# Building one quad's left factors later, reordering the last quad, and moving the weight sums in a two-layer graph kernel

## The chip, the cores and the metric

The kernel runs on one core of one Trainium2 chip. The metric is the device time of one execution in microseconds (us). Three runs of the kernel before took 2237.49, 2238.95 and 2239.25 us; their median, 2238.95, is the number against which the changed kernel stands. A further execution was taken by the hardware profiler; all lines of the trace come from it.

Five engines work side by side, each through its own list of instructions in order: TensorE (PE in the profile; PEld is its loading of stationary operands), VectorE (DVE), ScalarE (ACT), GpSimd (POOL) and SyncE (SP), which here only issues DMA transfers. POOL and ACT issue some transfers too.

## The reference

128 graphs, each with 128 nodes of 512 features, go through two layers. Everything is float32. Cut to what matters:

```python
# layer 0
h  = relu(layernorm(x))
Xw = h @ Wv + bv
e  = leaky_relu(sj[:, None, :] + si[:, :, None] + ab)      # sj, si = Xw @ the halves of aw
transition = adj * exp(e), each row divided by its sum
H = 0; Xk = h
for k in range(3):
    H  = H + Xk @ Wk[k] + bk[k]
    Xk = transition @ Xk
x = x + relu(H)
# layer 1
h    = relu(layernorm(x))
q, k = split(h @ Wqk);  v = h @ Wv
agg  = adj @ (k * mask)
w    = mask * sum(q * agg, axis=-1) / sqrt(512)            # one score per node
x    = x + softmax(w, over the nodes)[:, :, None] * v
```

The graphs don't touch each other. In layer 1 the scores of a graph need the product with the query and key weights, and the scaled values need the scores of the whole graph.

## The kernel before, in words

**Tiling.** Layer 0 goes over the graphs in 64 pairs (p = 0 to 63, some 21.6 us each), layer 1 in 32 quads (q = 0 to 31, two pairs each, some 24.5 us). A layer's large products are done by Strassen's scheme: a 2x2 block product with 7 block products instead of 8, from sums of blocks of the left operand and sums of blocks of the right one. Layer 1 uses the scheme twice, one inside the other: seven *outer* factors, numbered 1 to 7, each itself a product of seven *inner* ones. The outer factor's left operand is a sum of blocks of the normalised, transposed rows; the weight's sum is its right operand. PE's banks are eight tiles in PSUM, a1, b1, c1, e1 (set 1) and a2, b2, c2, e2 (set 2).

**Three kinds of preparation in layer 0.**

*Weight sums.* Layer 1's right operands are made once. In pairs 5 to 8, one VectorE step of 128x1024 each makes the outer sums (`combine_steps(*OUTER)`, tile `tl`). In pairs 9 to 15, one outer factor per pair, four steps of 128x256 (`prepare`, `combine_steps`, line 191, tile `stage`) make its four inner sums; `store_all` then puts them into DRAM (`rwd`) by four transfers on SP. From pair 16 on they are loaded back (`rw`). Where steps stand in VectorE's order is set by the main loop: with four steps, the first two stand in the `middle` of `statistics` of pair p+3 (behind its aggregate, ahead of the rest of its short arithmetic), the last two behind `for_layer1`, right ahead of the combination `x` (line 629) that ends the pair. A single step, in pairs 5 to 8, stands in that last place as well.

*Normalised rows for layer 1.* At the end of a pair `norm2` normalises the pair's result on ACT, stores it in DRAM (`h2d`) and has it loaded back in blocks of 32 rows (`by_blocks`: four loads of 128 KB on SP, tile `hv`). The blocks are there for a transposition: VectorE transposes 32x32 blocks, so that rows loaded in block order come out as a transposed tile.

*Left factors.* One pair later `for_layer1` transposes the blocks of that pair into `fw` (line 429, four transposes of 128x256). When both pairs of a quad are there, it makes the outer left factors: two sums, a store of the first half of the eight slots to DRAM (`fd`); then, in `upper`, two more sums and a store of the second half. The upper sums are made at the next quad's first pair. The stores are issued by POOL, except the second half of quad 30 and both halves of quad 31, which SP issues; quad 30's second half is slipped between the store of pair 63's rows and their load as blocks (`LAST`). In layer 1 `load_left` loads these factors back, 2 MB a quad, one quad ahead.

**What sets the order.** In layer 0 the kernel gives edges: `behind(what, op)` puts an operation behind the last one of that name (`tc.issue_after(done[what])`); all else follows the program's order and the data. In layer 1 each engine's list is the recorded order of calls: `put` chains every operation to the one before it on its engine (`dve`, `act`, `pool`, `sync`, `swdge`). PE's order is fixed by `ordered` in both layers.

**A quad of layer 1.** Two `one_round`s run side by side, one per bank set: in the first half of the quad the outer factors (1, 5) and (2, 6), in the second half (3, 7) and (4). A round has seven steps (products 1, 5, 6, 2, 7, 3, 4 with their copies and adds), and `together` runs the pair of rounds step by step; after step i it runs the work hooked to i. Into these hooks go the inner left sums of this quad (LATE) and the next one (EARLY), the loads of the next quad's rows and adjacency (`load_rest`), the softmax of the quad before (`peaks`, `exp_own`, `exp`, `factors`), the scaling of values by the softmax (`scale`, ACT), the addition of the residual (`add_x1`, a DMA that adds, issued by POOL) and the stores. `catch_up` opens a quad with the scores of the quad before and the loads of the next left factors. SBUF space comes from four pools `back[0]` to `back[3]`.

**The last quad** has an order of its own, written out by hand from line 1125 on: two rounds with two factors, (1, 6) and (2, 7), then the single factors 4, 5 and 3, with work of quads 29 and 30 in between. There its own scores, softmax and stores must follow quickly, for nothing else is left to cover them. The operations `u2`, `on_p5` and `from_u2` put part of the adding of factors onto POOL.

Of the kernel before, what the change touches and what calls it, by code (L numbers as in the profile page):

```python
# [16 lines left out]
def kernel(  # L17
# [28 lines left out]
    P = 128  # L46
# [287 lines left out]
    def by_blocks(h, hd=None, between=None):  # L334

        hd = dram.tile([G, P, D], FP, name="hd") if hd is None else hd
        nc.sync.dma_start(hd.rearrange("g n d -> n g d"), h)
        if between:
            between()
        hv = front.tile([P, G, Q, P], FP, name="hv")  # L340
        v = hd.rearrange("g (q b) (c i) -> c b (g q) i", b=S32, i=P)
        for c in range(DC):
            at = hv[c * S32:(c + 1) * S32].rearrange("p g q i -> p (g q) i")
            done["hv"] = nc.sync.dma_start(at, v[c]).ins  # L344
        return hv
# [69 lines left out]
    SUMS, LAST = {}, []  # L415

    def for_layer1(p):
# [13 lines left out]
        if second:  # L431
# [3 lines left out]
            def store_half(i):  # L435
                queue = nc.gpsimd if q + 1 + i < NQ else nc.sync
                half = slice(4 * i, 4 * i + 4)
                queue.dma_start(fd[:, half].rearrange("p o n -> p (o n)"), fv[:, half].rearrange("p o n -> p (o n)"))  # L438

            def upper():  # L440
                behind("c12", nc.vector.tensor_sub, at[7], at[1], fv[:, L21])
                done["c12"] = nc.vector.tensor_sub(at[3], at[2], at[6]).ins
                if q == NQ - 2:
                    LAST.append(partial(store_half, 1))
                else:
                    store_half(1)
# [5 lines left out]
            if q + 1 == NQ:  # L452
                SUMS.pop(q)()
# [179 lines left out]
    def norm2(p):  # L633

        if p not in RS2:
            norm2_statistics(p, "s7")
        rs = RS2.pop(p)
        h = behind("s7", norm_relu, X1[p], rs=rs)
        done["h2"] = done["h"]
        HV2[p] = by_blocks(h, H2D[p], LAST.pop() if p == NP - 1 else None)  # L640
# [60 lines left out]
    def inner_sums(q, factors, space=None):  # L701
# [3 lines left out]
        s = (space or early).tile([P, 4, n, N], FP, name=f"in{first}")  # L705
# [43 lines left out]
    for p in range(NP):  # L749
# [7 lines left out]
        def between():  # L757
            if p == 0:
                behind("t", norm0, 2)
                behind("rs", begin, 1)  # L760
                return
            if p + 2 < NP:
                behind("t", begin, p + 2)
            if p + 3 < NP:
                two = weights[:2] if len(weights) > 2 else []
# [15 lines left out]
        if p > 0:  # L781
            behind("c12", for_layer1, p - 1)
        for step in weights[-2:]:
            behind("c12", step)
            done["c12"] = done["right"]
# [51 lines left out]
    for_layer1(NP - 1)  # L837


# [31 lines left out]
    load_left(1, swdge)  # L871

# [163 lines left out]
    def catch_up(q, spread=True):  # L1036

        if q + 1 < NQ:
            load_left(q + 1, sync, (0,))
        scores(q - 1, 1, C[q - 1][:, 2])  # L1040
        if spread:
            PW[q - 1] = spread_scores(W[q - 1])
        if q + 1 < NQ:
# [23 lines left out]
    for q in range(NQ - 1):  # L1067
        if q:
# [5 lines left out]

        together(one_round(q, set1, (1, 5), s1, plain_ends(lambda i, j: c[:, 0:2, i, j])),
# [4 lines left out]
                  2: lambda: load_rest(q + 1, sync),  # L1080
                  3: work(*([lambda: scale(late, 1, 0)] if q > 1 else []),
# [14 lines left out]
        hooks = {3: sums[:2], 4: sums[2:]}  # L1096
# [16 lines left out]
        if q == NQ - 2:  # L1113
            sums = inner_sums(NQ - 1, LATE, back[3])
# [6 lines left out]
        if q > 1:  # L1121
            store(late, 1)
            C.pop(late)

# [7 lines left out]
    catch_up(q, False)  # L1132
# [9 lines left out]
    def u2(i, j):  # L1142
        pool(nc.gpsimd.tensor_add, c_(1, i, j), c_(0, i, j), c_(1, i, j))

    def on_p5(i):
        pool(nc.gpsimd.tensor_add, c[:, 2:4, i, 1], c[:, 0:2, i, 1], s2[:, 0].rearrange("p (k d) -> p k d", k=2))

    def from_u2(i, j):
        return lambda bank: dve(nc.vector.tensor_add, c[:, 2:4, i, j], bank, c[:, 0:2, i, j])

    def on_top(i, j):
        return lambda bank, t: in_place(c[:, 2:4, i, j])(bank)

    ra = one_round(q, set1, (1, 6), s1, plain_ends(lambda i, j: c[:, 0:2, i, j]), direct=True)
    rb = one_round(q, set2, (2, 7), s2, {(0, 0): from_u2(0, 0), (1, 1): on_top(1, 1), (0, 1): on_top(0, 1),
                                         (1, 0): from_u2(1, 0)}, direct=True)

    def a_h2(g):

        pair, j = divmod(g, 2)  # L1160
        bank = (a1, b1, c1, e1)[g]
# [14 lines left out]
    def score(pair, j, y):  # L1176
        junk = back[0].tile([P, D], FP, name="junk")
        b, at = (2 * q + pair) * G + j, pair * G + j
        dve(nc.vector.scalar_tensor_tensor, junk, AGG[q][:, j] if pair else (a1, b1)[j], wscale[:, b:b + 1],
# [6 lines left out]
    steps((ra, 0), (ra, 1), (ra, 2), (ra, 3))  # L1186
    u2(0, 0)
    scale(late, 1, 0)
    steps((rb, 0), (ra, 4))
    u2(1, 1)  # L1190
    scale(late, 1, 1)
    steps((ra, 5))
    u2(0, 1)
    soft[2] = spread_columns_of(W[prior], e1, 0, 2 * G)
    steps((rb, 1))
    exp_own(*soft[2])
    exp(*soft[2], 0)
    dve(nc.vector.tensor_add, outer(prior, 1), outer(prior, 3), outer(prior, 1))
    steps((ra, 6))
    u2(1, 0)  # L1200
    on_p5(1)
    on_p5(0)
    exp(*soft[2], 1)
    exp(*soft[2], 2)
    a_h2(0)
    steps((rb, 2))
    exp(*soft[2], 3)
    factors(*soft[2])
    add_x1(late, 1)
# [3 lines left out]
    a_h2(1)  # L1213
    a_h2(2)
    scale(prior, 1, 0)
    steps((rb, 4))
    a_h2(3)
    add_x1(prior, 0)
    scale(prior, 1, 1)
    add_x1(prior, 1)  # L1220
    steps((rb, 5))
    score(0, 0, c[:, 2])
    steps((rb, 6))
    score(0, 1, c[:, 2])
    for pair in range(2):
        store(late, pair)
    for pair in range(2):
        store(prior, pair)


    r4 = one_round(q, set2, (4,), s2, {
        (0, 0): lambda a: dve(nc.vector.tensor_add, c[:, 0:1, 0, 0], a, c[:, 3:4, 0, 0]),
        (1, 1): in_place(c[:, 0:1, 1, 1]), (0, 1): in_place(c[:, 0:1, 0, 1]),
        (1, 0): lambda a: dve(nc.vector.tensor_add, c[:, 0:1, 1, 0], a, c[:, 3:4, 1, 0])},
        early=lambda e: dve(nc.vector.tensor_add, c[:, 0, :, 1], e.to_broadcast([P, G, HD]), c[:, 3, :, 1]))
# [5 lines left out]
    r5 = one_round(q, set1, (5,), s1, {at: both(*at) for at in ((0, 0), (1, 1), (0, 1), (1, 0))}, direct=True)  # L1241

    def p5_of_r5():

        for k in (3, 1):
            pool(nc.gpsimd.tensor_add, c[:, k, :, 1], c[:, k, :, 1], s1[:, 0:1, :HD].to_broadcast([P, G, HD]))

    r3 = one_round(q, set2, (3,), s2, {at: in_place(c[:, 1:2, at[0], at[1]]) for at in ((0, 0), (1, 1), (0, 1), (1, 0))},
                   early=lambda e: dve(nc.vector.tensor_add, c[:, 1, :, 1], e.to_broadcast([P, G, HD]), c[:, 1, :, 1]))
# [7 lines left out]
    steps((r4, 0), (r4, 1), (r5, 0), (r5, 1))  # L1257
    p5_of_r5()
    soft[0] = spread_columns_of(W[q], e1, 0, G)
    steps((r4, 2), (r4, 3))  # L1260
    exp_own(*soft[0])
    exp(*soft[0], 0)
    exp(*soft[0], 1)
    steps((r4, 4), (r5, 2), (r4, 5))
    factors(*soft[0])
    steps((r5, 3), (r4, 6))
    score(1, 0, c[:, 0])
    score(1, 1, c[:, 0])
    steps((r5, 4), (r3, 0), (r5, 5), (r3, 1), (r5, 6), (r3, 2))
    soft[1] = spread_columns_of(W[q], a1, G, G)  # L1270
    exp_own(*soft[1])
    exp(*soft[1], 0)
    exp(*soft[1], 1)
    steps((r3, 3), (r3, 4), (r3, 5))
    finish(0, 0, c[:, 1, 0], nc.scalar)
    factors(*soft[1])
# [29 lines left out]
```

## Time and profile before

| what | value |
|---|---|
| median of three runs | 2238.95 us (2237.49 to 2239.25) |
| the profiled execution's own time | 2236.97 us |
| its span in the trace | 2235.2 us |
| mean granted clock of TensorE | 0.998 |
| busy: PE, DVE, ACT, POOL | 2207.0, 1658.9, 1235.8, 698.5 us |
| layer 0's weight sums (pairs 5 to 15) | about 170 to 405 us of the span |
| the step between the layers | about 1440 to 1480 us |
| last quad, first matmul | 2198.47 us |
| last quad, last matmul's end; VectorE's end | 2229.08; 2232.16 us |

How to read it: a line of the waits of PE names the waiting operation, the one it waited for, the total of us, the number of such waits and the longest. A line of the timeline gives the start, the duration, the engine, the line of the code, the operation, output<-input, the shape, how many in a row, and in square brackets the time the engine had been idle and what ended it. A line of the windows gives a stretch, its length, the busy time of PE, PEld, DVE, ACT and POOL (with counts), then the granted clock, the DMA engines' busy share and GB/s.

### The profile page before, as it was taken

How to read it: one execution, taken by the hardware profiler on the slowest of the kernel's cores; microseconds unless marked ns; L12 is line 12 of the kernel's file. 1: busy time of each engine (PE TensorE's matmuls, PEld its weight loads, DVE VectorE, ACT ScalarE, POOL GpSimd, SP SyncE). 2: the span in 40 equal slices, each digit the busy share in tenths (PEclk: the TensorE clock that was granted, in tenths of full speed). 3: DMA queues.
4: the chain of work that ended last, by engine and by line, in shares of the span. 5: the costliest groups of instructions: out<-in, count | busy, mean ns of one | idle time of the engine just before them, and what ended most of it. 6: DMA issues, size and time to landing. Idle time of an engine off the chain costs nothing.

```text
span 2235.2 us, 29424 instructions
## 1 busy us (share of the span) xinstructions
PE 2207.0 (99%) x8113; PEld 1536.1 (69%) x8113; DVE 1658.9 (74%) x4521; ACT 1235.8 (55%) x2858; POOL 698.5 (31%) x825
## 2 busy tenths in 40 slices
PE   9999999999999999999999999999999999999998
PEld 5666665656666666666666666678878888887886
DVE  5778777778777777777878777577777767777777
ACT  4555545555455555555555455456666666666664
POOL 2121111112121121212112121245555555555454
PEclk9999999999999999999999999999999999999999
DMA  7688788998788887887878786768888888888887
GB/s 199 178 246 245 228 264 253 269 273 247 226 232 233 227 241 218 243 232 228 241 225 237 224 236 200 270 222 235 220 250 231 240 221 249 237 233 239 242 229 206
DMA packets 426191, 523.54 MB, mean 234 GB/s; under 512 B 100374, under 2 KB 281238, under 8 KB 409642
## 3 DMA queue, kind: packets, MB, share of 16 engines
q1 hardware_dynamic: 384600, 397.08, 58.9%
q0 software_dynamic: 41136, 124.04, 21.3%
q8 instruction: 65, 1.06, 0.2%
q14 instruction: 100, 0.82, 0.1%
q10 hardware_dynamic: 290, 0.53, 0.1%
HBM read 297.35 MB, written 224.16 MB: 233 GB/s over the span
## 4 chain that ended last, share of the span: by engine, by line
PE 87%; DVE 5%; DMA 5%; SPq 2%; issue 1%; ACT 1%; DVEq 0%; POOL 0%; ACTq 0%
PE a L91 25%; PE b L91 23%; PE c L91 23%; PE e L91 15%; DMA td<-t 2%; DMA hv<-h2d 1%; SPq L542 1%; DMA tl<-in_L_gnn_Wqk_dram 1%; DVE fw L429 1%; SPq L344 0%; DMA h2d<-h 0%; DVE c L674 0%; SPq L86 0%; DVE x L629 0%; DVE st L290 0%
## 5 line engine op out<-in xcount | busy, mean ns | idle before, releaser
L674 POOL TENSOR_TENSOR c<-s,c 128x512 f32<-128x512 f32 (+1 forms) x186 | 199.9, 1089 | 258.5 <-DVE s L674 253.6
L111 POOL DMA_DIRECT2D agb<-in_adj_dram x256 | 149.7, 591 | 347.2 <-DVE aT L86 247.5
L91 PE MATMUL a<-r,x 128*128 128x512 f32 x512 | 240.8, 592 | 0.1
L91 PE MATMUL b<-rw,in 128*128 128x256 f32 x896 | 215.3, 379 | 1.7 <-ACT b L674 1.7
L91 PEld LDWEIGHTS b<-rw,in 128*128 128x128 f32 x896 | 170.0, 190 | 26.7 <-ACT b L674 2.8
L438 POOL DMA_DIRECT2D fd<-fw x61 | 34.1, 559 | 461.4 <-DVE fw L449 276.5
L91 PEld LDWEIGHTS a<-r,x 128*128 128x128 f32 x512 | 97.1, 190 | 96.2 <-issue 92.9
L86 ACT COPY s<-c 128x257 f32<-128x257 f32 (+1 forms) x128 | 61.4, 480 | 171.6 <-PE c L91 171.2
L86 ACT COPY b<-a 128x257 f32<-128x257 f32 (+1 forms) x128 | 59.3, 464 | 169.5 <-PE a L91 169.5
L86 DVE TENSOR_TENSOR e<-e,s 128x512 f32<-128x512 f32 x64 | 44.7, 698 | 144.1 <-ACT s L86 144.1
L674 POOL TENSOR_TENSOR c<-c 128x1024 f32<-128x1024 f32 (+1 forms) x65 | 146.2, 2249 | 15.7 <-DVE c L674 13.4
L91 PE MATMUL a<-w,x 128*128 128x257 f32 x512 | 131.9, 380 | 0.1
L91 PE MATMUL b<-w,sx 128*128 128x257 f32 x512 | 132.0, 380 | 0.0
L91 PE MATMUL b<-t,sx 128*128 128x512 f32 x256 | 120.4, 592 | 1.1 <-ACT b L86 1.1
L91 PE MATMUL c<-t,sx 128*128 128x512 f32 x256 | 120.3, 592 | 0.0
L91 PE MATMUL b<-r,sx 128*128 128x512 f32 x256 | 120.3, 592 | 0.0
L91 PE MATMUL c<-t,x 128*128 128x512 f32 x256 | 120.3, 592 | 0.0
L91 PE MATMUL e<-t,sx 128*128 128x512 f32 x256 | 120.3, 592 | 0.0
L674 ACT ACTIVATE c<-c,wcol 128x512 f32<-128x512 f32 x124 | 86.3, 719 | 60.4 <-DVE wcol L674 60.4
L674 DVE SCALAR_TENSOR_TENSOR junk<-agg,wscale,c 128x512 f32<-128x512 f32 x126 | 96.7, 768 | 29.8 <-POOL c L674 25.4
L429 DVE STREAM_TRANSPOSE fw<-hv 128x256 f32<-128x256 f32 x256 | 90.9, 412 | 35.7 <-DMA hv<-h2d 35.6
L91 PE MATMUL e<-rw,in 128*128 128x256 f32 x448 | 109.1, 383 | 3.1 <-DVE s L674 3.1
(257 smaller groups left out, 5240.1 us busy)
## 6 DMA issues: line engine op xcount, KB each, us to landing
fd<-fw POOLq DMA_DIRECT2D x61, 1024.0 KB, 5.1
x1d<-x SPq DMA_DIRECT2D x64, 512.0 KB, 5.7
h2d<-h SPq DMA_DIRECT2D x64, 512.0 KB, 3.1
hv<-h2d SPq DMA_DIRECT2D x256, 128.0 KB, 4.2
xg<-in_x_dram SPq DMA_DIRECT2D x63, 512.0 KB, 5.8
hd<-h SPq DMA_DIRECT2D x63, 512.0 KB, 3.1
hv<-hd SPq DMA_DIRECT2D x252, 128.0 KB, 3.5
h<-h2d SPq DMA_DIRECT2D x62, 512.0 KB, 8.7
```

The costliest lines, as they stand in the source:

```text
L86: return op(*args, **how)
L91: done["mm"] = op(*args, **how).ins
L111: nc.gpsimd.dma_start(agb[p][c * S32:(c + 1) * S32].rearrange("p g q i -> p (g q) i"), v[c])
L429: done["c12"] = nc.vector.transpose(blocks[:, k, j].rearrange("p f (n b) -> p f n b", n=Q), hv[:, j].rearrange("p n (k f a) -> p k f n a", ...
L438: queue.dma_start(fd[:, half].rearrange("p o n -> p (o n)"), fv[:, half].rearrange("p o n -> p (o n)"))
L542: done["tv"] = nc.sync.dma_start(tv[c * S32:(c + 1) * S32].rearrange("p g q i -> p (g q) i"), v[c]).ins
L674: done[engine] = op(*args, **how).ins
```

## The change

It has three parts.

1. *Weight sums.* Where a pair has four steps, the first two now stand behind `t` (the attention matrix of the pair after), ahead of `begin(p + 2)`, and the last two in the middle of `statistics`. A single step stands there as well. Behind `for_layer1` none is left.
2. *Left factors of quad 31.* Pairs 62 and 63 only store their normalised rows. `for_layer1` is called for pairs up to 61, so no transposes, sums or stores of quad 31 lie at the end of layer 0, and quad 30's upper sums take their place in the loop; its second store goes to POOL's queue. A tile `f31` in `back[3]` takes quad 31's factors: the blocks of pair 62 are loaded at the end of quad 1 and those of pair 63 at the end of quad 2 (`load_blocks`, SP), straight into slots 6 and 7 of that tile; they are transposed at hooks 4 and 6 of the first half of quads 2 and 3 (`block_transposes`, DVE), and the four sums are made at the same hooks of quads 4 and 5 (`last_left_sums`). The 2 MB load of quad 31's factors is gone. The EARLY sums of quad 1, made in quad 0, stand at hooks 2 and 4 instead of 3 and 4; the LATE sums of quad 31 go to `back[2]`.
3. *The last quad.* The rounds are (1, 2), then (6, 7) with factor 4 laid into its end, then 5 and 3. The first two `scale`s of quad 29 leave quad 30 and are done here. `catch_up` is replaced by the scores alone. The adds on POOL between factors become VectorE adds behind each bank (`first_copied`, `first_added`, `second_chained`, `second_added`), with two on POOL for one bank (`second_p5`). The softmax of the quad's first pair of graphs comes earlier, and the score columns use other banks.

The diff, cut to its core:

```diff
-    def by_blocks(h, hd=None, between=None):
+    def by_blocks(h, hd=None):
...
-        if between:
-            between()
...
             def store_half(i):
-                queue = nc.gpsimd if q + 1 + i < NQ else nc.sync
                 half = slice(4 * i, 4 * i + 4)
-                queue.dma_start(...)
+                nc.gpsimd.dma_start(...)
...
-            if q + 1 == NQ:
-                SUMS.pop(q)()
...
-        HV2[p] = by_blocks(h, H2D[p], LAST.pop() if p == NP - 1 else None)
+        if p < NP - 2:
+            HV2[p] = by_blocks(h, H2D[p])
+        else:
+            nc.sync.dma_start(H2D[p].rearrange("g n d -> n g d"), h)
...
+            if len(weights) > 1:
+                for step in weights[:2]:
+                    behind("t", step)
             if p + 2 < NP:
-                behind("t", begin, p + 2)
+                behind("right" if weights else "t", begin, p + 2)
             if p + 3 < NP:
-                two = weights[:2] if len(weights) > 2 else []
+                two = weights[-2:]
...
         if p > 0:
-            behind("c12", for_layer1, p - 1)
-        for step in weights[-2:]:
-            behind("c12", step)
-            done["c12"] = done["right"]
+            behind("c12", for_layer1 if p < NP - 1 else SUMS.pop(NQ - 2), *([p - 1] if p < NP - 1 else []))
...
-    for_layer1(NP - 1)
...
+    F[NQ - 1] = back[3].tile([P, 8, G, HC, N], FP, name="f31")
+
+    def load_blocks(p):
+        at = F[NQ - 1][:, 6:8].rearrange("p o j k n -> p o (j k n)")
+        v = H2D[p].rearrange("g (q b) (c i) -> c b (g q) i", b=S32, i=P)
+        for c in range(DC):
+            sync(at[c * S32:(c + 1) * S32].rearrange("p g (q i) -> p (g q) i", q=Q), v[c])
+        return at.rearrange("p g (q i) -> p g q i", q=Q)
+
+    def block_transposes(second, hv):          # four transposes, as in for_layer1
+    def last_left_sums():                      # four sums, as in for_layer1
...
-        if q + 1 < NQ:
+        if q + 1 < NQ - 1:
             load_left(q + 1, sync, (0,))
...
+        if q in (2, 3):
+            blocks = block_transposes(q - 2, HV2.pop(q))
+        elif q in (4, 5):
+            blocks = last_left_sums()[2 * (q - 4):2 * (q - 3)]
+        else:
+            blocks = []
...
+                  4: work(*blocks[::2]), 6: work(*blocks[1::2]),
...
-        hooks = {3: sums[:2], 4: sums[2:]}
+        hooks = {2: sums[:2], 4: sums[2:]}
...
         if q == NQ - 2:
-            sums = inner_sums(NQ - 1, LATE, back[3])
+            del hooks[5], hooks[6]
+            sums = inner_sums(NQ - 1, LATE, back[2].tile([P, 8, G, HC, N], FP, name="f"))
...
+        if 0 < q < 3:
+            HV2[q + 1] = load_blocks(2 * NQ - 3 + q)
...
-    catch_up(q, False)
+    scores(q - 1, 1, C[q - 1][:, 2])
...
-    ra = one_round(q, set1, (1, 6), s1, plain_ends(lambda i, j: c[:, 0:2, i, j]), direct=True)
-    rb = one_round(q, set2, (2, 7), s2, {(0, 0): from_u2(0, 0), (1, 1): on_top(1, 1), (0, 1): on_top(0, 1),
-                                         (1, 0): from_u2(1, 0)}, direct=True)
+    ra = one_round(q, set1, (1, 2), s1, {(0, 0): first_copied(0, 0), (1, 1): first_added(1, 1),
+                                         (0, 1): first_added(0, 1), (1, 0): first_copied(1, 0)}, direct=True)
+    rb = one_round(q, set2, (6, 7), s2, {(0, 0): second_chained(0, 0), (1, 1): second_added(1, 1),
+                                         (0, 1): second_added(0, 1), (1, 0): second_chained(1, 0)}, direct=True)
...
+    steps((ra, 0), (ra, 1))
+    scale(late, 0, 0)
+    a_h2(0)
+    steps((ra, 2))
+    scale(late, 0, 1)
...
+    soft[0] = spread_columns_of(W[q], a1, 0, G)
+    steps((rb, 1))
+    second_p5()
...
+    steps((r4, 0), (rb, 5))
+    scale(prior, 1, 0)
+    steps((r4, 2), (r4, 3), (rb, 6))
...
-    steps((r5, 4), (r3, 0), (r5, 5), (r3, 1), (r5, 6), (r3, 2))
-    soft[1] = spread_columns_of(W[q], a1, G, G)
+    steps((r5, 3), (r3, 0), (r5, 4), (r3, 1), (r5, 5))
+    soft[1] = spread_columns_of(W[q], a2, G, G)
     exp_own(*soft[1])
     exp(*soft[1], 0)
+    steps((r3, 2), (r3, 3), (r5, 6))
     exp(*soft[1], 1)
-    steps((r3, 3), (r3, 4), (r3, 5))
+    steps((r3, 4), (r3, 5))
+    factors(*soft[1])
     finish(0, 0, c[:, 1, 0], nc.scalar)
-    factors(*soft[1])
     finish(1, 0, c[:, 3, 0], nc.sync)
```

## The prediction, made before the changed kernel was run

> **What bounds the kernel now.** I read the page's first and fourth parts, then the waits of TensorE (PE) alone, then busy time by stage, then the timelines around the stages in which PE idles.
>
> ```profile
> PE 2207.0 (99%) x8113; PEld 1536.1 (69%) x8113; DVE 1658.9 (74%) x4521; ACT 1235.8 (55%) x2858; POOL 698.5 (31%) x825
> PE 87%; DVE 5%; DMA 5%; SPq 2%; issue 1%; ACT 1%; DVEq 0%; POOL 0%; ACTq 0%
> ...
> PE c L91 <- ACT s L86: 8.0, 7, 1.5
> PE e L91 <- DVE s L674: 3.1, 1, 3.1
> PE b L91 <- ACT b L674: 1.7, 2, 0.9
> ```
>
> PE sets the pace: 2207.0 of 2235.2 us. The change neither adds nor removes a matmul (both kernels issue the same 3137 matmul instructions), so it can win only PE's idle time, 28.2 us, a clock lost after an idle stretch, and what lies behind the last matmul. The waits (total, times, longest) name two targets: seven waits for ScalarE's copy `s` of layer 0, 8.0 us in all, and one of 3.1 us for VectorE's `s` of layer 1.
>
> ```profile
> 200.00:300.00 100.00, 98.50 (x321) 60.47 (x320) 78.86 (x248) 53.15 (x124) 19.41 (x34) 1.00 0.80 236
> 300.00:400.00 100.00, 95.48 (x325) 60.97 (x324) 75.50 (x239) 49.23 (x116) 16.83 (x29) 1.00 0.85 263
> 1460.00:1464.00 4.00, 3.32 (x8) 2.14 (x8) 4.00 (x6) 0.35 (x1) 2.68 (x3) 0.57 0.80 334
> 1500.00:2150.00 650.00, 650.00 (x2805) 532.62 (x2804) 467.36 (x928) 414.03 (x932) 356.68 (x290) 1.00 0.83 237
> 2200.00:2220.00 20.00, 18.21 (x77) 13.37 (x76) 12.79 (x26) 12.73 (x31) 13.40 (x15) 1.00 0.78 180
> ```
>
> By stage (busy us of PE, PEld, DVE, ACT, POOL; granted clock, DMA share, GB/s) PE idles while the weight factors are summed (1.50 us, 4.52, and 1.93 in 400 to 500), at the step between the layers, where the clock falls to 0.57 too, and in the last quad (1.79). From 1500 to 2150 it never idles: there nothing can be won, only lost.
>
> **Part 1, the weight sums.** In pairs 9 to 15 each pair issues four 128x256 `stage` steps of 0.42 us (0.33 from start to start). One of the seven stalls, VectorE's lines and PE's:
>
> ```profile
> 279.90 1.42 DVE L429 STREAM_TRANSPOSE fw<-hv 128x256 f32<-128x256 f32 x4 [1.69 <-DMA hv<-h2d]
> 282.70 0.42 DVE L191 TENSOR_TENSOR stage<-tl 128x256 f32<-128x256 f32 x1
> 283.03 0.42 DVE L191 TENSOR_TENSOR stage<-tl,stage 128x256 f32<-128x256 f32 x1
> 283.37 0.42 DVE L629 SCALAR_TENSOR_TENSOR x<-a,xg 128x256 f32<-128x256 f32 x1
> 295.53 1.29 DVE L290 BATCH_NORM_STATS2 st<-xg 128x6 f32<-128x512 f32 x2 [2.37 <-DMA xg<-in_x_dram]
> 288.18 1.14 PE L91 MATMUL c<-w,x 128*128 128x257 f32 x4 [1.50 <-ACT s L86]
> ```
>
> VectorE waits 1.69 us for the blocks `hv`, transposes them, adds twice, does two stage steps, then `x`, its statistics and `z`; ScalarE's exponential of `z` (287.18), the copies `y` and `s` follow, and PE waits for `s`. The two steps (282.70 to 283.37, 0.67 us) lie on that chain. The seven stalls are 1.50, 0.95, 1.18, 1.35, 1.04, 1.36 and 0.57; the last falls in pair 16, which has no stage steps, so about 0.6 of each belongs to something else: the chain goes round (`t`, its store and reload, then `hv`), and in these pairs SyncE also issues four weight-factor transfers. The change puts the two steps behind `t`, ahead of the transposes x<-hv, and the other two into the statistics, where two stood before. So what comes later is x<-hv and the sums behind it, by 4 x 0.42/2 = 0.8 us at most, and these feed a matmul one pair later; behind them VectorE idles for `xg` anyway (1.85, 2.37, 1.49, 2.77, 1.11, 2.52, 0.68 us in the seven pairs), which covers nearly all. In pairs 5 to 8 one step of 1.2 us sits on the same chain without a stall and moves to the statistics: worth nothing, its cover the same idle time. Saving: 7 x 0.67 = 4.7 us (the seventh stall has no step of its own, but inherits lateness). Bounds: 8.0 if all the stalls go, 0 if the transfers are the whole cause and merely wait longer. I take 4.7, nearest to the row that differs by just these steps (0.57 against a mean of 1.23, a difference of 0.66).
>
> **Part 2, the last quad's left factors.** Before, pair 63's normalised rows go to DRAM, come back as blocks, are transposed and summed four times on VectorE, between the layers:
>
> ```profile
> 1453.93 1.42 DVE L429 STREAM_TRANSPOSE fw<-hv 128x256 f32<-128x256 f32 x4 [3.22 <-DMA hv<-h2d]
> ...
> 1455.72 1.13 PE L91 MATMUL a<-rw,f 128*128 128x256 f32 x4 [0.65 <-DVE c L674]
> 1459.92 3.40 PE L91 MATMUL e<-rw,in 128*128 128x256 f32 x8 [3.07 <-DVE s L674]
> 1464.27 1.99 PE L91 MATMUL b<-rw,in 128*128 128x256 f32 x8 [0.94 <-ACT b L674]
> ```
>
> VectorE stands 3.22 us for `hv`, then 1.42 + 4 x 0.6 us of work, with layer 1's c, in and s queued behind. With the blocks read later all of it goes, 7.0 us off VectorE's queue, more than the stalls 0.65 + 3.07 + 0.94 = 4.66. The eight matmuls at 1459.92 took 3.40 us, the next eight, at nearly full clock, 1.99 (1.89 elsewhere): 1.5 us lost to the clock of 0.57. Sum 6.2. What can be late next: the first sums in<-f need the first half of `f`, whose loads landed at about 1447.8 to 1450.4, 14 to 16 us after issue, and are needed on VectorE from about 1448, at PE at 1455.1: up to 0.5 us; and ScalarE now writes pair 63's rows (1.52 us) ahead of the copy c<-b, which has about 0.5 us to spare: up to 1.0. Bounds: 4.0 (both, and the first stall kept) to 6.5; I take 6.2, because the largest wait has 7.0 us taken from ahead of it.
> The row says: clock 0.57 for about 4 us behind waits of 0.65 and 3.07. The Trainium skill, TensorE: Matmul & The Clock Gate, Part 1, has an idle window of about 3.4 us halve the clock until a busy window of the same length has passed. By the page, an estimate, the slow stretch costs up to 3.4/2 = 1.7 us instead of 1.5, and 3.07 us alone would be too short to trip it, so a part of the penalty could stay.
>
> What part 2 adds lies in quads 1 to 5: four loads of 128 KB at the end of quads 1 and 2 on SyncE (four such issues took 3.98 us at most; SyncE is idle 1510.96 to 1514.75), eight transposes of 0.41 us in the first rounds of quads 2 and 3, at hooks 4 and 6, and four sums of 0.68 us in those of quads 4 and 5. At hook 6 VectorE would wait for the spread scores anyway:
>
> ```profile
> 1500.16 0.69 DVE L674 TENSOR_REDUCE peak<-pw 128x4 f32<-128x512 f32 x1 [1.60 <-DMA pw<-pwd]
> ```
>
> (4.00, 2.33 and 2.18 us in three other quads), against 0.82 there. At hook 4 the copies behind have some 5 us to spare (s ready at 1472.5, wanted at 1477.5). Cost 0; if the cover is gone, four quads x 1.4 us = 5.6. Quads 29 and 30 lose 2 MB of loads, hidden: 0. Taking pair 30's second store from SyncE to POOL, between two loads: 0, up to 0.6 (POOL's mean issue, 559 ns).
>
> **Part 3, the last quad.** Before, PE waits 0.78, 1.00, 1.19 and 0.47 us there (3.44), and VectorE works until 3.08 us behind the last matmul (2229.08 to 2232.16). I walked the new order by hand with the same rows' durations (two matmuls 0.432, a 512-wide ScalarE copy 0.57, a scale 0.72, an exponential 0.35 and its read-out, a 512-wide VectorE add 0.60 to 0.69, a 256-wide 0.34 to 0.42, a score 0.78). The 0.78 goes, since no scale stands ahead of the first copy b. New waits: 0.1 and 0.3 around the first score columns, 0.6 where the second pair of factors' c copy stands behind two exponentials, 0.5 at the second score columns, 1.8 where the last factor's c copy stands behind exponentials that wait for VectorE's last peak, 0.2 elsewhere: 3.5 in all, as before. But the last softmax factors now precede the last matmuls, so behind these stand one add and two finishes (0.42 + 1.41 and a semaphore), 2.0 us instead of 3.08. Gain 1.1. Bounds -3 (ScalarE's in-order queue costs as much again as its two big waits, 0.6 and 1.8) to +2 (those two halved besides the gain).
>
> **Sum.** 4.7 + 6.2 + 1.1 = 12.0. The profiled execution took 2236.97 us, of which 2235.2 is its span; the median of the three runs, 2238.95, is 1.98 above. 2236.97 - 12.0 = 2224.97; plus 1.98 gives 2227.0 (0.53% faster). A measurement here tells about 0.2%, 4.5 us, from no change.
>
> **Rivals.** (a) The transfers hold the loop in layer 0. Then part 1 wins 1 to 2 us: 2230. For it: 0.57 us without a step, and `hv` awaited in each pair; against it: the steps stand in plain sequence behind that wait. (b) A wait takes the place of the one between the layers (loads of `f`, or ScalarE's order), and part 2 wins 3: 2230. For it: landings within 1 us of need; against it: 7.0 us leave the queue ahead. (a) and (b) together: 2233.5. (c) Little of it does what it says: the same lateness comes back behind the next wait and the whole is below 4.5 us: 2235 to 2239. (d) Slower: the loads of blocks at the end of quads 1 and 2 land late, and VectorE, in order, stands at hook 4 for them with `c` and `s` of that round queued behind. For it: such a load took 10 us between the layers (`h2d` out at 1438.97, `hv` at 1453.9); against it: hook 4 comes about 8 us behind the issue, with a median of 4.2 us to landing. Each us beyond the slack of 5 costs PE one in each of two quads, and the clock another 1.5 behind a wait of 3 or more: it decides from a delay of 11.75 us in each (2 x 6.75 + 2 x 1.5 = 16.5 us, against 12.0 + 4.5); at 14 us it gives 2227.0 + 21.0 = 2248.
>
> **How the numbers follow.** My sum within 3 us 0.50; (a) 0.14; (b) 0.12; both 0.06; (c) 0.10; (d) 0.08. The likeliest alone: 2223.5 to 2230. For 8 in 10, the low end is where part 1 ends all stalls and parts 2 and 3 reach their bounds half way (2222); the high end takes in (a), (b) and both: 2235. Faster by over 0.2% (below 2234.5): 0.50 + 0.14 + 0.12 + 0.06 + a little of (c) = 0.83; within 0.2% the rest of (c), 0.09; slower 0.08.
>
> **What the new profile would show.** Right: the waits of c for ACT s of L86 fall from 8.0 to about 3.3; no wait above 1 us between the layers and the clock at 1.00 there; PE still wholly busy from 1500 to 2150; some 2 us from the last matmul to VectorE's end. Wrong: stalls of 1 us in pairs 10 to 16 still, a wait for a load of `f`, idle PE in quads 2 to 5, or a wait above 2 us in the last quad.

## The result, and the profile after

The changed kernel takes 2229.96 us (median of five runs, 2227.59 to 2230.97), the kernel before 2239.25 (five runs, 2237.49 to 2240.99). The ratio is 0.9956, with a 95% interval of 0.9941 to 0.9970: it is faster by 0.44%, where 0.53% was forecast. The total came out near the forecast by a sum whose terms did not: of 4.7, 6.2 and 1.1 us, the first was wrong, the second slightly too small, the third much too large.

PE sends the same matmuls in the same order through both kernels until the last quad, so the start of one matmul in one trace can be set against the start of the same in the other. The first product of `y` and `tt` marks a pair of layer 0 (21.5375 us from one to the next where nothing stalls), the first product of `h` and `at` a quad of layer 1 (24.58 us). Worked out from the two profiled executions:

| stretch | before | after | difference |
|---|---|---|---|
| start of the program to pair 1 | 84.02 | 81.68 | -2.34 |
| pair 1 to pair 63 | 1341.98 | 1344.16 | +2.18 |
| of these, lost against 12 x 21.5375 from pair 8 to pair 20 | 9.84 | 11.57 | +1.73 |
| pair 63 to quad 0 | 15.54 | 15.54 | 0 |
| quad 0 to quad 1 | 31.47 | 24.59 | -6.88 |
| quad 1 to quad 30 | 712.96 | 712.96 | 0 |
| quad 30 to VectorE's last end | 46.19 | 45.90 | -0.29 |
| quad 30 to the end of the span | 49.23 | 49.25 | +0.02 |

The spans differ by 2235.2 - 2228.2 = 7.0 us. The first line is no part of the change (no instruction before pair 5 moved). That stretch ends on loads of weights that land at other times in each execution: over all the profiles of this study pair 1 starts between 80.67 and 84.02 us. It was lower in the kernels that hold part 2 (80.67 to 82.02, ten profiles) than in those that don't (82.90, 83.66 and 84.02); with three of the one kind this may be chance (by chance alone, three of thirteen would be the latest once in 286 orders), and it stays open. So 2.3 of the 7.0 us can't be put down to any part.

The waits of PE in the changed kernel (total, times, longest):

```profile
PE c L91 <- ACT s L86: 5.4, 4, 2.0
PE c L91 <- ACT c L669: 2.1, 2, 1.8
PE a L91 <- DVE tt L86: 1.8, 2, 1.2
...
PE a L91 <- DVE c L669: 1.3, 1, 1.3
PE b L91 <- ACT b L86: 1.2, 1, 1.2
```

The wait of 3.1 us between the layers is gone. The waits for `s` went from 8.0 us to 5.4, not to 3.3, and a wait that was not there before has come: for `tt`, the transposed attention matrix of layer 0. By stage (busy PE, PEld, DVE, ACT, POOL; granted clock, DMA share, GB/s):

```profile
300.00:400.00 100.00, 95.68 (x321) 60.75 (x320) 75.72 (x242) 49.40 (x118) 16.82 (x29) 0.98 0.86 258
400.00:500.00 100.00, 98.19 (x319) 60.00 (x319) 73.39 (x238) 52.76 (x123) 19.80 (x34) 1.00 0.89 269
...
1440.00:1460.00 20.00, 20.00 (x87) 16.10 (x86) 14.25 (x24) 9.54 (x19) 8.76 (x7) 1.00 0.76 307
1460.00:1480.00 20.00, 20.00 (x87) 16.10 (x86) 17.11 (x30) 11.33 (x28) 10.13 (x8) 1.00 0.58 165
1480.00:1500.00 20.00, 20.00 (x86) 16.12 (x85) 16.26 (x32) 13.23 (x31) 10.86 (x9) 1.00 0.85 251
1500.00:2150.00 650.00, 650.00 (x2807) 533.07 (x2807) 473.32 (x937) 413.88 (x922) 360.41 (x293) 1.00 0.83 236
```

In the weight stage PE idles as before (4.32 us from 300 to 400, where it was 4.52), and the clock is 0.98 there instead of 1.00. Between the layers PE is fully busy at clock 1.00. The work that part 2 adds to quads 1 to 5 costs nothing: 650.00 of 650.

### The profile page after: what moved, and what is told of

It is laid out like the page before. It is cut to its first block, busy times and chain, and to the rows that moved or that the text cites. A ratio compares the mean times of both kernels' runs of the same rounds, so it can differ in the third digit from the quotient of the medians.

```text
span 2228.2 us, 29421 instructions
## 1 busy us (share of the span) xinstructions
PE 2205.7 (99%) x8113; PEld 1535.0 (69%) x8113; DVE 1672.1 (75%) x4529; ACT 1235.8 (55%) x2858; POOL 698.6 (31%) x822
## 4 chain that ended last, share of the span: by engine, by line
PE 90%; DVE 4%; DMA 3%; SPq 1%; ACT 1%; issue 1%; DVEq 0%
PE a L91 26%; PE c L91 24%; PE b L91 24%; PE e L91 15%; DMA td<-t 2%; DMA hv<-h2d 1%; SPq L534 1%; DVE st L290 0%; DMA tl<-in_L_gnn_Wqk_dram 0%; DVE fw L427 0%; DVE z L86 0%; SPq L342 0%; DVE x L621 0%; DMA xg<-in_x_dram 0%; SPq L86 0%
## 5 line engine op out<-in xcount | busy, mean ns | idle before, releaser
L669 POOL TENSOR_TENSOR c<-c 128x1024 f32<-128x1024 f32 x61 | 144.1, 2362 | 11.2 <-DVE c L669 10.9
L91 PE MATMUL a<-rw,f 128*128 128x256 f32 x448 | 108.1, 379 | 0.0
```

The lines of the kernel that those rows point to most:

```text
L91: done["mm"] = op(*args, **how).ins
L669: done[engine] = op(*args, **how).ins
```

## Experiments

Theory A is the prediction's: the two weight steps ahead of `x` lie on the path that PE waits for, and part 1 wins 4.7 us. The rival B was its case (a): the transfers of these pairs hold the loop, and part 1 wins 1 to 2 us at most. The table gives for every kernel its median, its ratio to the kernel before with the 95% interval, and from its profile the stretches that matter ("lost": PE's lost time from pair 8 to pair 20).

| kernel | median us | ratio | lost | pair 1 to 63 | quad 0 to 1 | quad 30 to VectorE's end |
|---|---|---|---|---|---|---|
| before | 2237.9 to 2239.5 (four comparisons) | 1 | 9.84 | 1341.98 | 31.47 | 46.19 |
| changed | 2229.96 | 0.9956 (0.9941 to 0.9970) | 11.57 | 1344.16 | 24.59 | 45.90 |
| p1_only | 2239.3 | 0.9998 (0.9988 to 1.0009) | 9.93 | 1342.41 | 33.02 | 47.14 |
| no_p1 | 2231.7 | 0.9965 (0.9952 to 0.9978) | 10.07 | 1343.69 | 24.59 | 45.88 |
| no_p3 | 2227.95 | 0.9951 (0.9938 to 0.9964) | 9.77 | 1343.24 | 24.58 | 45.66 |
| p3_only | 2244.01 (one run) | | 14.59 | 1347.63 | 34.09 | 45.84 |
| rwd_one | 2223.37 | 0.9929 (0.9917 to 0.9940) | 4.88 | 1337.78 | 24.58 | 45.89 |
| rwd_pool | 2221.14 | 0.9912 (0.9898 to 0.9926) | 2.94 | 1335.48 | 24.71 | 45.89 |
| rwd_pool_old | 2223.26 | 0.9920 (0.9907 to 0.9933) | 3.00 | 1338.67 | 24.89 | 45.89 |
| rwd_pool_same | 2221.9 | 0.9921 (0.9906 to 0.9935) | 3.90 | 1338.06 | 24.59 | 45.91 |
| tail_copy | 2231.8 | 0.9960 (0.9946 to 0.9974) | 10.99 | 1345.80 | 24.59 | 44.97 |
| pool_tail | 2219.81 | 0.9914 (0.9901 to 0.9928) | 1.65 | 1334.98 | 24.59 | 44.98 |
| pool_mid_tail | 2217.18 | 0.9904 (0.9888 to 0.9919) | 0.09 | 1333.04 | 24.59 | 44.97 |

### One part alone, one part left out

**p1_only**: the kernel before with part 1.

```diff
+            if len(weights) > 1:
+                for step in weights[:2]:
+                    behind("t", step)
...
-                two = weights[:2] if len(weights) > 2 else []
+                two = weights[-2:]
...
-        for step in weights[-2:]:
-            behind("c12", step)
-            done["c12"] = done["right"]
```

> The kernel before with part 1 alone (the weight sums moved). If the steps lie on the chain that PE waits for, as predicted, it is 4.7 us faster than before: about 2234.5. If the transfers of pairs 9 to 16 hold the loop, it is the same: 2238 to 2241. In the two profiled executions, from the first matmul of y and tt of pair 1 to that of pair 63, 1341.98 us became 1344.16 us, 2.18 more: by this reading alone, 2241.4.

2239.3 us, ratio 0.9998 (0.9988 to 1.0009): no gain is seen from part 1 alone, and more than 2.7 us is excluded. Theory A's 4.7 us would be a ratio of 0.9979, outside the interval.

**no_p1**: the changed kernel with those lines as before.

> The changed kernel with the weight sums where they were before. If part 1 is worth 4.7 us, it is slower than the changed kernel by that: about 2234.7. If part 1 is worth nothing or costs 2 us, it is as fast or faster: 2227.8 to 2230.

2231.7 us, between the two expectations; its interval and that of the changed kernel overlap widely, so by the medians alone part 1 could be worth a few us here. In the profile it loses 10.07 us from pair 8 to pair 20, the changed kernel 11.57: there part 1 gains nothing here either, and what the profiles can put down to a part is almost all part 2's, 6.88 us.

**no_p3**: the changed kernel with the last quad's order of before.

> The changed kernel with the last quad's order of before (its own factor pairs, scales of quad 29 in quad 30). If part 3 gains 1.1 us as predicted, this is slower than the changed kernel by 1.1: 2231.1. By the two traces (33.69 us from the last quad's first matmul to VectorE's end before, 33.40 after; to the end of the span 36.73 and 36.77) it is the same: 2230.0.

2227.95 us: by the time, no gain of part 3 is seen. The stretch from quad 30 to VectorE's end is 45.66 us with the old order here, 46.19 in the kernel before and 47.14 in p1_only; with the new order it is 45.84 to 45.91 in seven profiles, **p3_only**, the kernel before with part 3 alone, among them. The new order is the steadier one. By the mean of the three old ones, 46.33, it gains 0.4 us, less than these differ among themselves (1.5 us): PE's first wait in the old order, which the new one doesn't have, was 0.78 us in the kernel before, 1.72 in p1_only, and missing in no_p3.

> The kernel before with part 3 alone. From the adjacency product of quad 30 to VectorE's end it was 46.19 us before and 45.90 in the changed kernel; predicted was 1.1 us less than before, 45.1, by the changed kernel's trace 45.9. Also read from it: the first product of y and tt of pair 1 starts at 83.7 to 84.0 us in the two profiles without part 2 and at 81.1 to 81.8 in the four with it; if that goes with part 2, 84 here; if it is chance, it may be 81.

45.84 us: the tail is the same with and without the other parts. Pair 1 starts at 82.90 us, between the two groups, which settles nothing on the start. This one run lost 14.59 us in the weight stage, with the step order of before: what the stage costs varies from run to run.

### What holds the weight stage

**rwd_one**: one factor is stored, seven times the same is loaded.

```diff
         def store_all():
+            if o != FACTORS[0]:
+                return
...
-            behind("x1d", nc.sync.dma_start, RW[o], RWD[o])
+            behind("x1d", nc.sync.dma_start, RW[o], RWD[FACTORS[0]])
```

> The changed kernel with the sums of one factor alone stored to DRAM, in pair 9, and all seven right operands of layer 1 loaded from that one; the sums of the other six are made on VectorE and left unstored, so the result uses a wrong weight. If those transfers hold the loop, PE's stalls in pairs 10 to 16 (11.6 us of lost time from pair 8 to 20 in the changed kernel) fall to under 3 us and the time to about 2221. If the steps on VectorE and the rest of the chain hold it, it stays within 2 us of the changed kernel, 2228 to 2230.

2223.37 us, 6.6 below the changed kernel: rival B. The loss is 4.88 us, more than the 3 that were expected. All weight steps are still made; only pair 9 stores. PE loses 2.51 us from the mark of pair 10 to that of pair 11, behind pair 9's stores, and at most 0.68 us from any other to the next.

**rwd_pool**: POOL issues those stores.

```diff
-            behind("x1d", nc.sync.dma_start, RWD[o][:, :4], t)
+            behind("x1d", nc.gpsimd.dma_start, RWD[o][:, :4], t)
...
-                behind("x1d", nc.sync.dma_start, RWD[o][:, 4 + i], r[at])
+                behind("x1d", nc.gpsimd.dma_start, RWD[o][:, 4 + i], r[at])
```

> The changed kernel with the stores of the right operands (rwd) issued by POOL instead of SP. POOL's list puts the three unchanged blocks of each factor into pairs up to 9 and leaves one store of 512 KB per pair from 9 to 15; the bytes are the same in all. If the stalls come from these transfers standing ahead of x and t's store on SP's queue and on the DMA engines, the 11.6 us lost from pair 8 to 20 fall below 5 and the time to 2223. If it is the mere amount of traffic in layer 0, it stays at 2228 to 2230.

2221.14 us, 8.8 below the changed kernel, with every byte stored. This put the unchanged blocks into earlier pairs as well. **rwd_pool_same** holds them in their own pairs:

```diff
+            done["rwd"] = behind("x1d", nc.gpsimd.dma_start, RWD[o][:, :4], t).ins
...
+                behind("rwd", nc.gpsimd.dma_start, RWD[o][:, 4 + i], r[at])
```

> The changed kernel with the stores of the right operands on POOL as before, but each factor's three unchanged blocks held behind its stage store, so that all four transfers stay in their own pair, 9 to 15. If SP's queue was what made them harmful (4 issues between the stores of x and of t), the lost time between pairs 8 and 20 stays near 3 us and the time near 2221. If the amount in one pair is what counts, the loss is back at 10 us or more: 2228 to 2230.

2221.9 us and 3.90 us lost: the amount per pair is not what counts; what counts is where and when the four stores are issued. First the changed kernel's SyncE queue ahead of the mark of pair 15, then the same place in this kernel:

```profile
374.21 0.45 SPq L623 DMA_DIRECT2D x1d<-x  x1
374.71 1.47 SPq L86 DMA_DIRECT2D rwd<-stage  x1
376.22 3.98 SPq L86 DMA_DIRECT2D rwd<-tl  x3
380.25 0.47 SPq L101 DMA_DIRECT2D xg<-in_x_dram  x1
380.82 0.46 SPq L529 DMA_DIRECT2D td<-t  x1
...
386.55 1.81 SPq L534 DMA_DIRECT2D junk<-td  x4
```

```profile
373.64 0.66 SPq L101 DMA_DIRECT2D xg<-in_x_dram  x1
375.20 0.36 SPq L529 DMA_DIRECT2D td<-t  x1
376.47 0.36 SPq L337 DMA_DIRECT2D h2d<-h  x1
...
379.99 1.80 SPq L534 DMA_DIRECT2D junk<-td  x4
```

POOL issues the stores here behind that reload:

```profile
383.18 0.55 POOL L86 DMA_DIRECT2D rwd<-stage  x1
383.72 1.60 POOL L86 DMA_DIRECT2D rwd<-tl  x3
```

The rows of `t` and of its way back, in the timeline of the changed kernel and in that of this one:

```profile
378.61 0.48 DVE L521 TENSOR_SCALAR t<-z,d 128x128 f32<-128x128 f32 x2
391.43 0.45 DVE L86 STREAM_TRANSPOSE tt<-junk 128x256 f32<-128x256 f32 x1 [1.62 <-DMA junk<-td]
391.93 0.70 PE L91 MATMUL a<-y,tt 128*128 128x256 f32 x2 [1.20 <-DVE tt L86]
```

```profile
374.69 0.48 DVE L521 TENSOR_SCALAR t<-z,d 128x128 f32<-128x128 f32 x2
385.63 0.43 DVE L86 STREAM_TRANSPOSE tt<-junk 128x256 f32<-128x256 f32 x1
```

In the changed kernel `t` is ready at 379.09, but SyncE issues its store only at 380.82, for the four weight stores take 374.71 to 380.20; the reload `junk` follows at 386.55 (5.73 us later), and `tt` starts 12.3 us after `t`. PE waits for it. With the stores on POOL's queue `td` goes out at 375.20, 0.03 us after `t`, the reload 4.79 us later, and `tt` starts 10.5 us after `t`. In the weight pairs the median from issue to landing of td<-t is 5.7 us in the changed kernel, 4.0 in this one. So two things sat ahead of `t` in this pair: 1.7 us of waiting for the queue, and about a further microsecond in the transfer.

Over all seven pairs with stores (those that end at the marks of pairs 10 to 16), worked out from the rows of `t`, td<-t and junk<-td:

| kernel | weight steps, stores | `t` ready, `td` not yet issued: sum of seven | from td's issue to the reload's: mean |
|---|---|---|---|
| before | old place, SyncE | 2.83 | 5.47 |
| no_p1 | old, SyncE | 4.21 | 5.49 |
| changed | new, SyncE | 7.69 | 5.59 |
| p1_only | new, SyncE | 8.84 | 5.49 |
| rwd_pool_same | new, POOL | 0.19 | 4.10 |
| rwd_pool_old | old, POOL | 0.20 | 4.36 |

Where no such store is made, `td` waits 0.03 us and the reload follows after some 3.5 us. Between two kernels that differ in part 1 alone, `t` stood longer for the queue with part 1 by 6.0 us (p1_only against the kernel before) and by 3.5 us (the changed kernel against no_p1), 4.7 in the mean: about what part 1 had taken out ahead of `x` came back as waiting for the queue. The kernel before at the same place:

```profile
376.98 1.30 SPq L86 DMA_DIRECT2D rwd<-stage  x1
378.32 3.72 SPq L86 DMA_DIRECT2D rwd<-tl  x3
...
382.61 0.48 SPq L537 DMA_DIRECT2D td<-t  x1
...
387.86 1.80 SPq L542 DMA_DIRECT2D junk<-td  x4
```

The queue is the smaller of the two delays in the kernel before (0.4 us a pair against about 2 us more from the issue of `td` to the reload). Moving the stores to POOL took them off SyncE's queue and behind the reload at once, so that the runs don't tell the queue from the moment at which the bytes move. Behind `td` on the same queue come the rows `h2d`, and behind them the blocks for VectorE's transposes, on which the chain to PE's other wait, for `s`, hangs.

**rwd_pool_old**: rwd_pool with the steps where they were before.

> The same with the weight sums where they were before the change. If the two steps ahead of x are on PE's path once the transfers are out of the way, as the prediction had it, 0.67 us is lost in each of seven pairs, and this is 4.7 us slower than the kernel with the stores on POOL and the new places. If the new places have a price of their own (0.4 us a pair, as in pair 8 of the changed kernel: VectorE's statistics of xg come 0.8 us later, ScalarE's logarithm waits for them, and the copy c<-b, for which PE waits, stands behind it), the two differ by less than 2 us.

2223.26 us against 2221.14. The intervals overlap, and from pair 8 to pair 20 the two lose the same, 3.00 and 2.94 us: theory A's 4.7 us isn't there even when the transfers are out of the way. The 3.2 us by which its profile is longer from pair 1 to 63 lie elsewhere, in pairs 2, 6, 20 and 61 for the most part (0.70, 1.03, 1.05 and 0.64). A stall in pair 6, where a single step stands, came in two of the four profiles with the steps where they were before (1.03, and 0.38 in no_p1) and in none of the nine others, so part 1 may be worth something there; no run singles it out.

### The price of the new place

Part 1 cost 0.40 us from the mark of pair 8 to that of pair 9, where nothing stalled before, and rwd_pool shows the same 0.41, 0.41 and 0.40 behind the marks of pairs 8, 12 and 14. All eight profiles with two steps behind `t` lose 0.40 or 0.41 at pair 8; of the others, three lose nothing there and two 0.66 and 0.84 (rwd_pool_old, p3_only). VectorE, then ScalarE, then PE in the changed kernel:

```profile
243.04 0.42 DVE L191 TENSOR_TENSOR stage<-rl,stage 128x256 f32<-128x256 f32 x1
...
246.54 1.28 DVE L290 BATCH_NORM_STATS2 st<-xg 128x6 f32<-128x512 f32 x2
247.74 0.30 DVE L291 BATCH_NORM_AGGREGATE mv<-st 128x2 f32<-128x6 f32 x2
```

```profile
248.07 0.29 ACT L86 ACTIVATE r<-mv,eps 128x2 f32<-128x2 f32 x1 [1.84 <-DVE mv L291]
248.39 0.20 ACT L296 ACTIVATE r<-r 128x2 f32<-128x2 f32 x1
248.50 0.58 ACT L86 COPY c<-b 128x512 f32<-128x512 f32 x1
```

```profile
247.12 1.88 PE L91 MATMUL a<-r,x 128*128 128x512 f32 x4
249.14 1.98 PE L91 MATMUL c<-t,sx 128*128 128x512 f32 x4
```

The two steps behind `t` push the statistics of `xg` back; ScalarE stands 1.84 us for their result, and the copy c<-b, which PE's next matmul needs, is queued behind. VectorE didn't idle for `xg` here at all: in this pair the load was early, and the cover that the prediction named was not there.

**pool_tail** and **pool_mid_tail** put the pieces together: the first is the changed kernel with the edits of rwd_pool and of tail_copy (told below). The second moves, besides, all weight steps into the middle of the statistics, behind the aggregate that ScalarE waits for:

```diff
-            if len(weights) > 1:
-                for step in weights[:2]:
-                    behind("t", step)
...
-                two = weights[-2:]
+                two = weights
```

> The changed kernel with both gains so far: the stores of the right operands on POOL, and the last factor's product and copy ahead of the last softmax's exponentials. The first took 11.6 us of lost time to 2.9 between pairs 8 and 20, the second shortened the way from quad 30's adjacency product to VectorE's end from 45.90 to 44.97: together 2220.2, 19 us below the kernel before.

> The same with all weight steps in the middle of the statistics (none behind t). If the 0.41 us lost in pairs 8, 12 and 14 and the 1.27 in pair 10 come from the two steps behind t, which hold up the statistics of xg, ScalarE's logarithm and the copy c<-b queued behind it, most of these 2.5 us goes: 2218. If they come from elsewhere, it is the same as the kernel without this move; if the four steps hold up the normalisation instead, it is slower by up to 3.

2219.81 and 2217.18 us. In pool_tail the loss is 0.41 in each of pairs 8, 10, 12 and 14 and nothing else; with the steps behind the aggregate it is 0.09 in all. The weight stage of pool_mid_tail, and its waits:

```profile
270.00:440.00 170.00, 170.00 (x572) 108.03 (x571) 136.73 (x434) 90.59 (x213) 35.28 (x61) 1.00 0.85 258
```

```profile
PE c L91 <- DVE c L669: 1.4, 1, 1.4
PE a L91 <- DVE c L669: 1.3, 1, 1.3
PE b L91 <- ACT b L86: 1.2, 1, 1.2
```

PE is busy for all of the stage at a DMA share of 0.85, the same share as in the changed kernel (0.85, with 162.79 us of 170 busy): the share of busy DMA engines told nothing of what was late. This version is 0.96% faster than the kernel before (0.81 to 1.12%) and 12.8 us below the changed one by the medians.

### The last quad

**tail_copy**:

```diff
     soft[1] = spread_columns_of(W[q], a2, G, G)
+    steps((r3, 2),)
     exp_own(*soft[1])
     exp(*soft[1], 0)
-    steps((r3, 2), (r3, 3), (r5, 6))
+    steps((r3, 3), (r5, 6))
```

> The changed kernel with one step of the last factor moved: the product whose bank ScalarE copies (c<-b) is called ahead of the exponentials of the last softmax instead of behind the first of them; PE's order is the same. If PE's last wait, 1.84 us for that copy, is due to the exponentials ahead of it, the wait goes, and VectorE's end behind the last matmul sets the rest: 1 to 1.8 us faster than the changed kernel, 2228.5. If the products of that factor wait for something else then, it is the same.

The time, 2231.8, can't tell it from the changed kernel, because the weight stage varies by more. The stretch itself can: 45.90 us becomes 44.97, 0.93 less, and 44.98 and 44.97 in the two kernels that take it over. The changed kernel's end, ScalarE's and VectorE's rows around PE's last wait:

```profile
2218.43 0.42 DVE L669 TENSOR_REDUCE peak<-a 128x2 f32<-128x256 f32 x1
...
2219.07 0.20 ACT L669 ACTIVATE wcol<-wcol 128x2 f32<-128x2 f32 x1 [4.91 <-DVE wcol L669]
2219.18 0.35 ACT L669 ACTIVATE ej<-a,peak 128x128 f32<-128x128 f32 x1
...
2219.52 0.37 ACT L669 COPY c<-b 128x256 f32<-128x256 f32 x1
...
2219.95 0.70 PE L91 MATMUL c<-rw,f 128*128 128x256 f32 x2 [1.84 <-ACT c L669]
...
2223.42 1.41 DVE L669 SCALAR_TENSOR_TENSOR h<-c,wcol,h 128x512 f32<-128x512 f32 x2
```

and that of tail_copy:

```profile
2219.25 0.36 ACT L669 COPY c<-b 128x256 f32<-128x256 f32 x1 [3.11 <-PE b L91]
...
2222.32 0.70 PE L91 MATMUL c<-rw,f 128*128 128x256 f32 x2 [1.39 <-DVE c L669]
```

ScalarE stood 4.91 us for VectorE's peak with the copy behind it. With the copy ahead, PE's wait for it is gone, and the next one takes over half of the gain: PE's last product waits 1.39 us for VectorE, which works through its queue without a break.

## Why the prediction was right or wrong

**The total** lies in the range, but not by its terms. 12.0 us were summed; what the profiles put down to the three parts is 0 + 6.9 + 0.3 = 7.2; the medians differ by 9.3. The 2 us between are not accounted for: the start of the program, the weight stage and, without part 2, the stretch between the layers all vary between executions. That a sum whose second largest term is missing still lands 3.0 us from the median is luck, and 2229.96 is also what rivals (a) and (b) had each named, 2230. One of the prediction's own signs of being wrong came: stalls of 1 us in pairs 10 to 16 are still there.

**Part 2, 6.2 us: right, a little small.** 6.88 us went between quad 0 and quad 1, and all the stalls named for it. The clock stayed at 1.00, so the slow stretch behind the wait went with it, as the row of 3.40 us against 1.99 had it. In the two other kernels without part 2 the stretch is longer still (33.02 and 34.09 us), so that it saves 6.9 to 9.5 us by these profiles. That may be one reason why the medians differ by more than the spans; it was not tested. The doubt drawn from the Trainium skill (TensorE: Matmul & The Clock Gate, Part 1), that a part of the slow clock could remain, found nothing to act on there: no idle stretch was left. The rival (b) did not come: VectorE stands 0.96 us for the loads of `f` at 1447.24, at the place named, and PE doesn't notice:

```profile
1447.24 0.69 DVE L669 TENSOR_TENSOR in<-f 128x512 f32<-128x512 f32 x1 [0.96 <-DMA f<-fd]
```

The work in quads 1 to 5 was free, and rival (d) with it is out: PE is fully busy from quad 1 to quad 30, in 712.96 us in both kernels. What spoke for (d) was misread: the 10 us between the layers lie between the store of the rows (1438.97) and the issue of their load (1449.18), and the load itself was in by 1453.93.

**Part 1, 4.7 us: wrong.** The step that failed is "the two steps lie on that chain", priced at 7 x 0.67. They do stand between the transposes and `x`, and after the change `x` follows the sums at once; but the chain is a loop through `t`, its store, its reload and `hv`, and what lengthens the loop in these pairs are the four stores ahead of `td`: with them out of its way the 11.57 us fall to 3.90 and 2.94, and with the steps in the old place 10.07 fall to 3.00. Taking 0.67 us out of one place let `t` wait about as much longer for SyncE's queue (4.7 us over the seven pairs), and PE wait for `tt`, which it had not done before. The row that the prediction leaned on, 0.57 us in the pair without steps against a mean of 1.23, has another reading that p1_only and rwd_pool_old bear out: the stalls follow the stores, and that was the first pair behind the last of them. The kernel before's own trace had the counterpart: two steps stand right ahead of `x` at 257.95 to 258.68, before the first store (262.52), and PE lost nothing behind that mark, pair 9's. The second step that failed is "VectorE idles for `xg` anyway, which covers nearly all": the cover was read from pairs in which `xg` came late because of the same stores. Where the load is early, the price is 0.41 us (pool_tail: in pairs 8, 10, 12 and 14), and it passes through ScalarE: the prediction had looked at who reads x<-hv, not at who waits for the statistics behind it and what is queued there. Rival (a) was right in its mechanism, and named it ("The transfers hold the loop"), but was given 0.14; it too allowed part 1 more (1 to 2 us) than the runs show.

**Part 3, 1.1 us: too large.** PE's waits in the last quad were walked as 3.5 us and are 0.28 + 1.31 + 1.84 = 3.43, the largest at the place and of the size named; the agreement of the sum is partly luck, for 1.31 at the second score columns had been put at 0.5. What failed is "2.0 us behind the last matmul": it is 2.97 (2221.86 to 2224.83), hardly less than the 3.08 of all three profiles with the old order. Behind PE's last wait VectorE still has two adds, the softmax factors, two finishes, an add and two finishes in line, and the last matmul is not what it waits for. The term measured 0.3 us in the two profiles and 0.4 by the mean of the old order's three, which range from 0.2 us below the new order to 1.2 above.

## What to carry to other kernels

A stall that comes round in every iteration belongs to a loop, not to the instruction ahead of it: before an instruction is priced by its duration, follow the loop once round, through each queue's issues, and ask what else gives way when this one goes. Transfers with time to spare don't belong ahead of one that a loop waits for; moving four such stores a pair from SyncE's queue to POOL's, where they came later, was worth 8.1 and 8.8 us here by the medians, nearly as much as the whole change. Where work is moved into an idle stretch, look who waits for what comes behind it on that engine, and what is queued behind the waiter.

## What was not expected of the hardware

Four issues on SyncE took 3.4 to 5.5 us in a row in the changed kernel's pairs 9 to 15 (in layer 1, loads of blocks into `f`, 4.07 and 2.54 us) and held a ready store for 0.6 to 1.7 us, while the busy share of the DMA engines was the same 0.85 with the stalls and without them. The kernel before varied by 10 to 12 us from run to run within a comparison (2234.81 to 2246.61, 2236.62 to 2247.06, 2233.52 to 2245.80); the kernels without the stalls of the weight stage stayed within about 2 us (pool_tail 2219.01 to 2220.76, pool_mid_tail 2216.65 to 2218.64), though in 5 and 4 runs against 11 to 19.

An idle stretch of 2.04 us was enough to lower the granted clock: behind the changed kernel's longest stall it is 0.50 for the next two microseconds and the four matmuls that take 1.88 us elsewhere took 3.50, which made this stall cost 4.01 us instead of 2.04. The Trainium skill (TensorE: Matmul & The Clock Gate, Part 1) speaks of an idle window of some 3.4 us that runs freely; where the two differ the measurement decides, and a stall of 2 us is priced at about twice its length here. The stalls of 1.08 and 1.20 us had no such tail, nor had one of 1.50 in the kernel before (it cost 1.77) or one of 1.84 in the last quad (clock 1.00 behind it); one of 2.39 us in p3_only cost 4.35, with the clock at 0.50 there too. First PE's rows, then the stretches around it (busy PE, PEld, DVE, ACT, POOL; granted clock, DMA share, GB/s):

```profile
331.46 1.26 PE L91 MATMUL c<-w,x 128*128 128x257 f32 x4 [2.04 <-ACT s L86]
332.51 3.50 PE L91 MATMUL a<-r,x 128*128 128x512 f32 x4
335.85 1.88 PE L91 MATMUL e<-t,sx 128*128 128x512 f32 x4
```

```profile
331.00:333.00 2.00, 1.54 (x5) 1.22 (x6) 1.79 (x13) 2.00 (x5) 1.93 (x4) 0.84 1.02 404
333.00:335.00 2.00, 2.00 (x3) 0.67 (x2) 1.97 (x6) 1.12 (x3) 0.53 (x2) 0.50 0.88 276
335.00:337.00 2.00, 2.00 (x5) 0.91 (x4) 1.93 (x6) 0.90 (x3) 0.47 (x1) 0.81 1.00 319
```
